# Four image layers on one core: the scan's tiles in a pool of their own, and the Toeplitz rows of two convolutions loaded into its place

## The chip, the core and the metric

The kernel runs on one core of one Trainium2 chip. The metric is device time in microseconds (us) from the start of the program to its end; it is given as the median of repeated executions. A core has five engines that run in parallel, each through its own list of instructions in order: TensorE (PE; its weight loads are shown apart as PEld), VectorE (DVE), ScalarE (ACT), GpSimd (POOL) and SyncE (SP). DMA transfers are issued from the lists of SP, ACT and POOL and run on 16 DMA engines. An engine that meets a wait in its list does nothing behind it until the wait is over.

## The reference

The input is x of 8 x 384 x 32 x 32 in f32. Four layers follow one another:

- Layer 0: an RMS norm, a selective scan over the 1,024 pixels of an image in both directions (16 states for each of 384 channels), and a gated 3x3 depthwise convolution.
- Layer 1: 1x1 and depthwise convolutions, a linear attention with 8 heads, and an MLP of width 1,536.
- Layer 2: the sum of seven depthwise convolutions, each with its batch norm.
- Layer 3: a 1x1 convolution with residual, a 13x13 depthwise convolution plus a scaled copy, and a GELU.

Cut to layers 2 and 3, in which the change mostly lies:

```
# layer 2: kernels of 13, 5, 7, 7, 3, 3, 3 with dilations 1, 1, 1, 2, 3, 4, 5
out = bn(dwconv(x, w_lk, 1))
for w, r in zip(branches, dilates):
    out = out + bn(dwconv(x, w, r))
# layer 3
y    = einsum('bchw,oc->bohw', x, pw_w)
x_pw = bn(y) + x
out  = bn(dwconv13(x_pw, dwk_w)) + bn(x_pw * dw1_w)
return gelu(out)
```

A depthwise convolution has one small kernel per channel and mixes no channels. The seven kernels of layer 2 fit into one 13x13 kernel per channel, and the scaled copy of layer 3 into the middle tap of its 13x13 kernel.

## The kernel before, in words

**Layers 0 and 1** (`_layers01`, L361 to L1119) go image by image. `front(b)` makes the inputs of the scan of image b, `scan(b)` does the scan, `layer1(b)` the rest. A loop at L1094 walks through the scan's steps, and between two steps takes pieces of `front` of the next image and `layer1` of the last one, by costs and due times (L1103 to L1115). After the last scan, `layer1` of the last image runs alone (L1117). All tiles of these layers come from one SBUF pool, `sp` (L376): among them those of the scan, `bct` (4 buffers), `rep` (6), `da` (4) and `hs` (8), each of 4 KB per partition.

Some steps of `layer1` matter below. It loads `g`, the result of the scan (L884); multiplies it with a matrix (`op`); makes the image `hh` with a border, whose two edge columns a POOL memset clears (L526) and whose middle ScalarE fills (L899); writes `hh` to DRAM (`put_image`, L532); reads it back as shifted copies `dw_i` (24 loads, L543); and ends by writing its result `xx` into the DRAM image `x2_d` from POOL (L1070), three writes for each half image.

**The convolutions** (L235 to L358) are done by TensorE with Toeplitz matrices, for all 8 images together. For one channel, the 32 rows of the image at 4 horizontal shifts fill 128 partitions. The weights for one group of taps are a 32-column matrix that holds the kernel along its diagonals; they come as windows out of a DRAM table (`g2_d`, `g3_d`), which was filled early on (`kernels`, L164). Four channels share one PSUM tile, so 384 channels make 96 groups of 32 recorded matmuls each.

`conv` (L264) takes 16 channels (four groups) as a block. For each block:

- POOL loads the block's image rows into `xt` (L281, 626 KB); two VectorE copies make the other three shifts (L289).
- SP and ACT load the windows into `tp` (L287), four transfers of 256 KB, two from each queue.
- TensorE does the groups (L301), and `put` takes the result of each out of PSUM, which has six tiles for it (`cps`).

`xt` and `tp` have three buffers each. In the first convolution ("a", layer 2), `put2` copies each group from PSUM into `yt`, ScalarE and VectorE in turn (L315, L317), and POOL writes four groups at once to `y2_d` (L319). In the second ("b", layer 3), `put3` applies GELU on ScalarE into one of three tiles `ot` (L353), and POOL writes each to the output (L354).

Between the two is the pointwise stage (L326 to L347): SP loads `yp` from `y2_d` (L328), TensorE multiplies (L333), ScalarE and VectorE finish, and POOL writes `xp_d` (L347), the image that convolution b reads. Its bias `pbias` is computed by 18 recorded matmuls before convolution a (L251 to L262).

**What sets the order.** The tile framework records the program, plans the order of each engine's list, and places the tiles of a pool in SBUF. A tile that reuses a buffer waits for the last user of that buffer. A pool that takes the place of a closed one waits, with the default setting, for the users of the closed pool as a whole. In the built program each transfer of POOL also waits for the POOL transfer eight before it, and each of SP and ACT for the one of the same queue four before it, in the convolutions.

Of the kernel before, what the change touches and what calls it, by code (L numbers as in the profile page):

```python
# [10 lines left out]
FP = mybir.dt.float32  # L11
AF = mybir.ActivationFunctionType
ALU = mybir.AluOpType
# [3 lines left out]
P = 128  # L17
C = 384
NC = C // P
H = 32  # L20
# [17 lines left out]
IMG = (H + 2) * (W + 2)  # L38

N_A6, N_T2, N_S2, N_W, N_IM = 7, 9, 3, 4, 8  # L40
N_REP, N_DA, N_HS = 6, 4, 8
AHEAD = 5000
TP = H * KT
# [24 lines left out]
def tile_layers(  # L68
# [78 lines left out]
    def bns(name, c):  # L147
        i = _BN.index(name)
        return bn_s[:, c, i : i + 1]
# [14 lines left out]
    def kernels(small, large):  # L164
# [60 lines left out]
        with nc.allow_non_contiguous_dma(reason="384 biases"):  # L225
            nc.gpsimd.dma_start(bias_d.rearrange("(c p) -> p c", p=P), bias3[:, :, 0])
            nc.gpsimd.dma_start(biasq_d, bias_d.rearrange("(g q) -> q g", q=4))
        yield 1

    _layers01(tc, nc, B, xv, x2_d, dram, ident, mean_w, eps5, eps6, one, half, minus1, vec, bns, bnt,  # L230
              rs, rsm, inproj_t, xproj_t, dtproj_t, outproj_t, taps1, taps3, taps3b, sel, alog,
              cw1_t, cw2_t, qkv_t, proj_t, w1, w2, headmask, mask8, mask8_t, kernels)


    NQ = C // 4  # L235
    GB = 4
    with tc.tile_pool(name="cw", bufs=1) as cwp, tc.tile_pool(name="cx", bufs=2) as cxp, tc.tile_pool(
        name="cps", bufs=6, space=PSUM
    ) as cps:
        xos = []  # L240
        for i in range(3):
# [5 lines left out]
        gbias = cwp.tile([P, NQ], FP, tag="gbias", name="gbias")  # L247
        for q in range(4):
            nc.scalar.dma_start(gbias[q * H : (q + 1) * H, :], biasq_d[q, :].partition_broadcast(H))

        pbias = cwp.tile([P, NC, 1], FP, tag="pbias", name="pbias")  # L251
        for m in range(NC):
            ps = cps.tile([P, HALF], FP, tag="cv", name=f"pb_{m}")
            for k in range(NC):
                nc.tensor.matmul(
                    ps[:, 0:1], pwt[:, k, m * P : (m + 1) * P], bias2[:, k, :],
                    start=(k == 0), stop=(k == NC - 1),
                )
            nc.vector.scalar_tensor_tensor(
                pbias[:, m, :], ps[:, 0:1], bns("pw", m), bnt("pw", m), ALU.mult, ALU.add  # L260
            )
            nc.vector.tensor_add(pbias[:, m, :], pbias[:, m, :], bias2[:, m, :])  # L262

        def conv(g_d, src_d, tag, put):  # L264

            NCH = 4 * GB
            xt = tp = None
            for g in range(NQ):  # L270
                if g % GB == 0:
                    xt = cxp.tile([P, NCH, RL], FP, tag="xt", name=f"xt_{tag}_{g}", bufs=3)
                    tp = cxp.tile([P, NCH, TP], FP, tag="tp", name=f"tp_{tag}_{g}", bufs=3)

                    q0 = g // GB % 2 * 2
                    at = [H * ((q0 + e) % NSH) for e in range(NSH)]
                    src = bass.AP(
                        src_d.tensor, src_d[4 * g, 0, 0].offset,
                        [[RL, H], [H * RL, NCH], [1, RL]],
                    )  # L280
                    nc.gpsimd.dma_start(xt[at[0] : at[0] + H], src)  # L281
                    for e in range(NSH):
                        win = bass.AP(
                            g_d.tensor, g_d[4 * g, e, 0, 0].offset,
                            [[KT, H], [NSH * TG * KT, NCH], [1, TP]],
                        )
                        (nc.scalar if e % 2 else nc.sync).dma_start(tp[at[e] : at[e] + H], win)  # L287
                    for n in (1, 2):
                        nc.vector.tensor_copy(  # L289
                            xt[at[n] : at[n] + n * H, :, 0 : RL - n - (n - 1)],  # L290
                            xt[at[0] : at[0] + n * H, :, n : RL - (n - 1)],
                        )
                ps = cps.tile([P, HALF], FP, tag="cv", name=f"cv_{tag}_{g}")
                for t in range(KT):
                    for e in range(4):
                        c = 4 * (g % GB) + e
                        row = xt[:, c, NSH * t : NSH * t + B * (W + PADW) - PADW]
                        rhs = bass.AP(
                            row.tensor, row.offset, [row.ap[0], [W + PADW, B], [1, W]]
                        )  # L300
                        nc.tensor.matmul(  # L301
                            ps[H * e : H * (e + 1), 0:BW],
                            tp[:, c, :].rearrange("p (j t) -> p j t", t=KT)[:, :, t], rhs,
                            start=(t == 0), stop=(t == KT - 1), skip_group_check=True,
                        )
                put(g, ps[:, 0:BW])
# [13 lines left out]

        conv(g2_d, x2_d, "a", put2)

        yf = y2_d.rearrange("(k p) h b w -> p k (h b w)", p=P)
        xf = xp_d.rearrange("(k p) h r -> p k h r", p=P)
        NB = 2 * BW
        for t in range(H // 2):  # L326
# [3 lines left out]
            for m in range(NC):  # L330
# [10 lines left out]
                for r in range(2):  # L341
# [3 lines left out]
                        yt[:, m, r * BW : (r + 1) * BW].rearrange("p (b w) -> p b w", w=W),  # L345
                    )
            nc.gpsimd.dma_start(xf[:, :, 2 * t : 2 * t + 2, :], xo)  # L347

        ov = out.rearrange("b c h w -> (c h) b w")

# [9 lines left out]

def _layers01(tc, nc, B, xv, x2_d, dram, ident, mean_w, eps5, eps6, one, half, minus1, vec, bns, bnt,  # L361
              rs, rsm, inproj_t, xproj_t, dtproj_t, outproj_t, taps1, taps3, taps3b, sel, alog,
              cw1_t, cw2_t, qkv_t, proj_t, w1, w2, headmask, mask8, mask8_t, kernels):

# [7 lines left out]
    with ExitStack() as ctx:  # L374
        wp = ctx.enter_context(tc.tile_pool(name="w0", bufs=1))
        sp = ctx.enter_context(tc.tile_pool(name="s0", bufs=2))  # L376
        accp = ctx.enter_context(tc.tile_pool(name="acc0", bufs=1, space=PSUM))
        psp = ctx.enter_context(tc.tile_pool(name="ps0", bufs=3, space=PSUM))

# [315 lines left out]
        def scan(b):  # L695
# [9 lines left out]

            def load_bc(k, r):
                d, h, _ = units[k]
                t = sp.tile([P, 2, HALF], FP, tag="bct", name=f"bct_{b}_{d}_{h}_{r}", bufs=4)
                for o in range(2):
                    src = bass.AP(  # L710
                        bc_d.tensor, bc_d[b, d, o * NST + 4 * r, h * HALF].offset,
                        [[0, 32], [L, 4], [1, HALF]],
                    )
                    nc.sync.dma_start(t[:, o, :], src)
                return t

            def load(k, i):
# [1 line left out]
                d, h, c = units[k]  # L719
                ts = []  # L720
                for src_d, n in ((dl_d, "dlt"), (v_d, "vr")):
                    t = sp.tile([P, 2 * HALF], FP, tag="rep", name=f"{n}_{b}_{d}_{h}_{c}_{i}", bufs=N_REP)
                    for j in range(2):
                        src = bass.AP(
                            src_d.tensor, src_d[b, d, P * c + 32 * (2 * i + j), h * HALF].offset,
# [35 lines left out]
            for k, (d, h, c) in enumerate(units):  # L761
                cols = bass.ts(h, HALF)
                second = k % (2 * NC) >= NC
                for r in range(NR):
# [11 lines left out]
                    end = HALF - 1 if d == 0 else 0  # L776
                    for i in range(2):
                        dlt, vt = now[i]
                        da = sp.tile([P, 2 * HALF], FP, tag="da", name=f"da_{b}_{k}_{r}_{i}", bufs=N_DA)
                        for j in range(2):  # L780
                            g = 4 * c + 2 * i + j
                            nc.scalar.activation(  # L782
# [9 lines left out]
                            sums(*late.pop(0))  # L792
                        if i == 0 and k and c == 0 and r == 0:
                            bct[NR - 1] = load_bc(k, NR - 1)
                        t = sp.tile([P, 2 * HALF], FP, tag="hs", name=f"hs_{b}_{k}_{r}_{i}", bufs=N_HS)
                        for j in range(2):
                            s = bass.ts(j, HALF)
                            k_c = carry[:, c * NR + r, 2 * i + j : 2 * i + j + 1]
# [295 lines left out]
        for b in range(B):  # L1094
            for i, _ in enumerate(scan(b)):
# [7 lines left out]
                while True:  # L1103
# [10 lines left out]
                    else:  # L1114
                        w[4] += cost  # L1115
        tick(everything=True)
        for _ in seconds[B - 1]:  # L1117
            tick()
        tick(everything=True)  # L1119


# [86 lines left out]
```

## Time and profile before

Three executions took 5239.56 us in the median (5237.00 to 5242.91).

| what | us |
|---|---|
| the profiled execution | 5247.45 |
| its span, first to last instruction | 5245.7 |
| TensorE busy | 4292.2 (82%) |
| VectorE busy | 3793.6 (72%) |
| GpSimd busy | 2911.7 (56%) |
| ScalarE busy | 2739.8 (52%) |
| the last scan's last matmul | at 4220.2 |
| layer 1 of the last image, alone | 4220 to 4558 |
| first matmul of convolution a | at 4594.75 |
| first matmul of the pointwise stage | at 4827.8 |
| first matmul of convolution b | at 4971.5 |

Times inside the profile are counted from the start of the span. A row of a group of instructions names the line, the engine and the operation, then the tile written and the tile read; after the bar it gives busy time and the mean of one, then how long the engine was idle just before it and what ended that wait. A row of waits reads "who <- whom: us in total, times, longest". A row of the timeline has start, duration, engine and line, and in brackets the idle time before it. For a DMA issued by POOL the shown duration is that of the issue; its landing is listed apart.

### The profile page before, as it was taken

What the parts mean: (1) busy time and instruction counts of PE and PEld (TensorE: products, weight loads), DVE (VectorE), ACT (ScalarE), POOL (GpSimd) and SP (SyncE); (2) the same over time, 40 slices, a digit from 0 to 9 for tenths busy, and PEclk for the clock granted to TensorE, in tenths of its full rate; (3) what the DMA queues carried; (4) which work ended last, traced back from release to release, by engine and by line L of the source; (5) the groups of instructions that cost most, each with busy time, mean ns of one, the idle gap of its engine ahead of it and who ended that gap; (6) DMA issues with size and microseconds to landing.
All of it is one profiled execution on the core that took longest, in us unless ns stands there. A gap on an engine that the chain in (4) does not pass through costs nothing. (4 is left out here: it accounts for less than half of the span.)

```text
span 5245.7 us, 57987 instructions
## 1 busy us (share of the span) xinstructions
PE 4292.2 (82%) x20128; PEld 1772.1 (34%) x20128; DVE 3793.6 (72%) x3765; ACT 2739.8 (52%) x3816; POOL 2911.7 (56%) x1472
## 2 busy tenths in 40 slices
PE   4675568888988998898889888998788879787877
PEld 1121123233333333333333333333233324365455
DVE  0399899987888788878887889788879901065344
ACT  1455544785578557755775677468536603001211
POOL 3276666676667665766675667566767800111155
PEclk7686679899989998999899999999889999899988
DMA  9866447666757674767567646765644541499698
GB/s 280 253 198 209 167 146 217 205 202 177 213 190 208 177 222 168 224 179 218 176 199 203 213 168 196 211 204 183 160 150 137 147 105 38 79 235 219 193 197 168
DMA packets 560045, 975.07 MB, mean 186 GB/s; under 512 B 53208, under 2 KB 238024, under 8 KB 559752
## 3 DMA queue, kind: packets, MB, share of 16 engines
q1 hardware_dynamic: 410992, 669.13, 42.8%
q0 software_dynamic: 56800, 205.10, 15.2%
q10 hardware_dynamic: 91960, 97.14, 6.8%
q8 instruction: 159, 2.61, 0.2%
q14 instruction: 134, 1.10, 0.1%
HBM read 726.36 MB, written 244.81 MB: 185 GB/s over the span
## 5 line engine op out<-in xcount | busy, mean ns | idle before, releaser
L808 POOL TENSOR_TENSOR hs<-hs,bct 128x1024 f32<-128x1024 f32 x768 | 2410.7, 3139 | 1001.1 <-DVE carry L804 470.6
L782 ACT ACTIVATE da<-dlt,neg_a 128x512 f32<-128x512 f32 x1536 | 1035.6, 715 | 775.7 <-DVE hs L799 718.5
L799 DVE TENSOR_TENSOR_SCAN hs<-da,du 128x512 f32<-128x512 f32 x768 | 902.4, 1209 | 248.7 <-ACT da L782 146.3
L787 DVE TENSOR_TENSOR du<-vr,bct 128x1024 f32<-128x1024 f32 x768 | 1059.3, 1379 | 29.0 <-DMA vr<-v_d 18.5
L799 DVE TENSOR_TENSOR_SCAN hs<-da,carry,du 128x512 f32<-128x512 f32 x768 | 944.1, 1267 | 56.4 <-PE acc L506 14.4
L506 PE MATMUL acc<-hs,selt 128*32 128x512 f32 x2304 | 560.5, 658 | 189.8 <-POOL hs L808 189.7
L1058 PE MATMUL mo<-hm,w 128*128 128x512 f32 x1152 | 572.0, 637 | 91.1 <-ACT hm L1056 89.4
L489 PE MATMUL mf<-ln,w 128*128 128x512 f32 x1152 | 565.6, 627 | 11.7 <-DMA w<-w_d 11.7
L501 PE MATMUL acc<-hs,selt 128*32 128x512 f32 x768 | 419.5, 645 | 72.8 <-POOL hs L808 46.8
L1058 PEld LDWEIGHTS mo<-hm,w 128*128 128x128 f32 x1152 | 219.4, 200 | 438.3 <-issue 240.3
L782 ACT ACT_TABLE_LOAD x278 | 356.7, 1283 | 7.6 <-ACT hh L899 2.7
L489 PEld LDWEIGHTS mf<-ln,w 128*128 128x128 f32 x1152 | 222.4, 200 | 334.3 <-issue 314.3
L489 PE MATMUL in<-xn,win 128*128 128x512 f32 x576 | 293.0, 640 | 12.0 <-ACT uz L603 7.7
L301 PE MATMUL cv_b<-xt_b,tp_b 128*32 128x256 f32 x3072 | 203.9, 424 | 83.3 <-ACT ot L353 60.6
L1070 POOL DMA_DIRECT2D x_d<-xx x48 | 56.4, 1177 | 350.6 <-DVE xx L1067 350.5
L289 DVE COPY xt_b<-xt_b 32x4992 f32<-32x4992 f32 (+1 forms) x48 | 135.0, 2813 | 131.8 <-DMA xt_b<-xp_d 131.0
L1056 ACT ACTIVATE hm<-mf,biasf 128x512 f32<-128x512 f32 x192 | 131.9, 687 | 179.6 <-PE mf L489 177.8
L301 PE MATMUL cv_a<-xt_a,tp_a 128*32 128x256 f32 x3072 | 182.3, 389 | 47.0 <-issue 37.1
L506 PE MATMUL dw<-dw_i,t3b 96*32 96x512 f32 x1056 | 207.5, 637 | 4.1 <-DMA dw_i<-h_d 3.6
L301 PEld LDWEIGHTS cv_b<-xt_b,tp_b 128*32 128x32 f32 x3072 | 150.8, 143 | 136.8 <-ACT ot L353 71.2
L506 PEld LDWEIGHTS acc<-hs,selt 128*32 128x32 f32 x2304 | 92.7, 114 | 301.3 <-POOL hs L808 281.0
L354 POOL DMA_DIRECT2D out<-ot x96 | 130.4, 1363 | 113.4 <-ACT ot L353 113.1
(194 smaller groups left out, 5771.4 us busy)
## 6 DMA issues: line engine op xcount, KB each, us to landing
dlt<-dl_d SPq DMA_DIRECT2D x384, 256.0 KB, 4.2
vr<-v_d SPq DMA_DIRECT2D x384, 256.0 KB, 4.9
bct<-bc_d SPq DMA_DIRECT2D x256, 256.0 KB, 3.8
ut<-u_d SPq DMA_DIRECT2D x192, 257.5 KB, 5.6
lc_i<-xn_d SPq DMA_DIRECT2D x192, 228.8 KB, 5.5
dw_i<-h_d SPq DMA_DIRECT2D x192, 228.8 KB, 4.5
w<-w_d SPq DMA_DIRECT2D x64, 576.0 KB, 6.1
w<-in_w SPq DMA_DIRECT2D x64, 576.0 KB, 5.4
```

The source lines that it names most:

```text
L289: nc.vector.tensor_copy(xt[at[n] : at[n] + n * H, :, 0 : RL - n - (n - 1)], xt[at[0] : at[0] + n * H, :, n : RL - (n - 1)],)
L301: nc.tensor.matmul(ps[H * e : H * (e + 1), 0:BW], tp[:, c, :].rearrange("p (j t) -> p j t", t=KT)[:, :, t], rhs, start=(t == 0), stop=(t = ...
L354: nc.gpsimd.dma_start(ov[g * P : (g + 1) * P], ot.rearrange("p (b w) -> p b w", w=W))
L489: nc.tensor.matmul(ps, w[:, k, m * P : (m + 1) * P], rhs[k] if isinstance(rhs, list) else rhs[:, k, :], start=(k == 0), stop=(k == NC - 1),)
L501: first = product()
L506: tc.keep_in_program_order(product())
L782: nc.scalar.activation(da[:, bass.ts(j, HALF)], dlt[:, bass.ts(j, HALF)], AF.Exp, scale=neg_a[:, g, r : r + 1],)
L787: nc.vector.tensor_mul(pairs(du), pairs(vt), bct[r][:, 0:1, :].to_broadcast([P, 2, HALF]),)
L799: nc.vector.tensor_tensor_scan(t[:, s][:, way], da[:, s][:, way], du[:, s][:, way], k_c if second else 0.0, ALU.mult, ALU.add,)
L808: made.append(nc.gpsimd.tensor_mul(pairs(t), pairs(t), bct[r][:, 1:2, :].to_broadcast([P, 2, HALF])))
L1056: nc.scalar.activation(hm, ps, AF.Gelu, bias=biasf[:, NC * i + f, :])
L1058: nc.tensor.matmul(acc[m], wb[:, f, m * P : (m + 1) * P], hm, start=(i == 0 and f == 0), stop=(i == FF // C - 1 and f == NC - 1),)
```

## The change

Four things change.

1. The scan's tiles (`bct`, `rep`, `da`, `hs`) come from a pool of their own, `scan`, placed at the right end of SBUF. It is closed when the last scan has ended. In its place a pool `win` of 20 buffers `tp` is opened, each with the windows of 8 channels (4 KB per partition).
2. During `layer1` of the last image, the first 20 window tiles of convolution a are loaded by POOL, one tile (four transfers) after each step of `layer1`. In the pointwise stage one window tile of convolution b is loaded after each of the 16 steps, by ACT and SP. Inside `conv`, windows are loaded up to ten blocks ahead.
3. `conv` takes 8 channels as a block in place of 16, with four buffers `xt` in place of three.
4. The pools of the convolutions wait tile by tile for the memory that they take over (`reuse_waits="tile"`). `pbias` is computed after convolution a.

The framework plans the order of each list anew. In the built program of the changed kernel, the windows of convolution b with numbers 0 to 19 stand in the lists of SP and ACT ahead of the pointwise stage, each behind the block of convolution a that frees its buffer.

```diff
+N_WIN, NCH = 20, 8
...
+    def load_windows(g_d, tag, n, queues):
+        if not wins:
+            wins["pool"] = ctx.enter_context(tc.tile_pool(name="win", bufs=1, side="right"))
+        tp = wins["pool"].tile([P, NCH, TP], FP, tag="tp", name=f"tp_{tag}_{n}", bufs=N_WIN)
+        for e in range(NSH):
+            at = H * ((n % 2 * 2 + e) % NSH)
+            win = bass.AP(
+                g_d.tensor, g_d[NCH * n, e, 0, 0].offset,
+                [[KT, H], [NSH * TG * KT, NCH], [1, TP]],
+            )
+            queues[e % len(queues)].dma_start(tp[at : at + H], win)
+        wins[tag, n] = tp
+
+    def windows(queues):
+        for n in range(N_WIN):
+            load_windows(g2_d, "a", n, queues)
+            yield
...
-    with tc.tile_pool(name="cw", bufs=1) as cwp, tc.tile_pool(name="cx", bufs=2) as cxp, tc.tile_pool(
-        name="cps", bufs=6, space=PSUM
+    with tc.tile_pool(name="cw", bufs=1, reuse_waits="tile") as cwp, tc.tile_pool(
+        name="cx", bufs=2, reuse_waits="tile"
+    ) as cxp, tc.tile_pool(
+        name="cps", bufs=6, space=PSUM, reuse_waits="tile"
     ) as cps:
...
         def conv(g_d, src_d, tag, put):
-            NCH = 4 * GB
             for g in range(NQ):
-                if g % GB == 0:
-                    xt = cxp.tile([P, NCH, RL], FP, tag="xt", name=f"xt_{tag}_{g}", bufs=3)
-                    tp = cxp.tile([P, NCH, TP], FP, tag="tp", name=f"tp_{tag}_{g}", bufs=3)
+                n, first = divmod(4 * g, NCH)
+                if first == 0:
+                    xt = cxp.tile([P, NCH, RL], FP, tag="xt", name=f"xt_{tag}_{n}", bufs=4)
...
+                    for m in range(n, min(n + 1 + N_WIN // 2, NB_C)):
+                        if (tag, m) not in wins:
+                            load_windows(g_d, tag, m, [nc.sync, nc.scalar])
+                    tp = wins[tag, n]
...
             nc.gpsimd.dma_start(xf[:, :, 2 * t : 2 * t + 2, :], xo)
+            if t < N_WIN:
+                load_windows(g3_d, "b", t, [nc.scalar, nc.sync])
...
+        scan_ctx = ExitStack()
+        scanp = scan_ctx.enter_context(tc.tile_pool(name="scan", bufs=1, side="right"))
...
-                t = sp.tile([P, 2, HALF], FP, tag="bct", name=f"bct_{b}_{d}_{h}_{r}", bufs=4)
+                t = scanp.tile([P, 2, HALF], FP, tag="bct", name=f"bct_{b}_{d}_{h}_{r}", bufs=4)
...
         tick(everything=True)
+
+        scan_ctx.close()
+        ahead = windows([nc.gpsimd])
         for _ in seconds[B - 1]:
             tick()
+            next(ahead, None)
+        for _ in ahead:
+            pass
         tick(everything=True)
```

The same replacement of `sp.tile` by `scanp.tile` is made for `rep`, `da` and `hs`, and the block that computes `pbias` moves behind the call of `conv` for convolution a.

## The prediction

> **What bounds the kernel now.** I read the page first (TensorE busy 82%, VectorE 72%, no engine full everywhere), then cut the span into stages, since the diff only touches what follows the last scan. The table of stages (start:end, length, then busy time of PE, PEld, DVE, ACT, POOL, TensorE clock, DMA share, GB/s):
>
> ```profile
> 4220.00:4558.00 338.00, 300.66 (x896) 129.95 (x888) 31.63 (x46) 66.32 (x107) 8.89 (x13) 0.94 0.30 70
> 4558.00:4594.70 36.70, 3.97 (x18) 3.91 (x18) 8.73 (x9) 0.00 (x0) 8.47 (x8) 0.55 0.89 135
> 4594.70:4814.00 219.30, 182.14 (x3072) 157.22 (x3072) 143.18 (x94) 17.50 (x47) 40.85 (x44) 0.98 1.11 235
> 4814.00:4827.80 13.80, 0.15 (x1) 0.00 (x0) 0.00 (x0) 0.37 (x1) 0.75 (x1) 0.62 0.77 192
> 4827.80:4953.00 125.20, 125.16 (x288) 55.30 (x288) 35.83 (x94) 36.55 (x47) 11.26 (x15) 0.99 0.65 208
> 4953.00:4971.50 18.50, 0.28 (x1) 0.01 (x1) 6.30 (x5) 0.78 (x1) 2.72 (x4) 0.62 0.64 156
> 4971.50:5240.50 269.00, 203.90 (x3072) 150.78 (x3072) 129.50 (x46) 45.01 (x95) 147.05 (x116) 0.88 0.94 179
> ```
>
> The rows are: the last image's layer 1, TensorE-bound with the DMA 30% used; an empty gap; convolution a; a gap; the pointwise stage, TensorE without a hole; a gap; convolution b. Convolution a has its DMA queues full (1.11: packets overlap, so the share can pass 1). Its TensorE needs 182 of 219 us; what it waits for is seen in the timeline of one block of 16 channels:
>
> ```profile
> 4704.24 1.25 POOL L319 DMA_DIRECT2D y_d<-yt  x1 [7.32 <-ACT yt L315]
> 4705.48 0.67 POOL L281 DMA_DIRECT2D xt_a<-x_d  x1
> ...
> 4711.36 2.73 DVE L289 COPY xt_a<-xt_a 64x4960 f32<-64x4960 f32 x1
> ...
> 4714.19 7.46 PE L301 MATMUL cv_a<-xt_a,tp_a 128*32 128x256 f32 x128 [1.43 <-issue]
> 4714.38 0.67 POOL L281 DMA_DIRECT2D xt_a<-x_d  x1
> ```
>
> TensorE starts at 4714.19, when the second VectorE copy ends (4714.09). The block's input was asked for at 4696.25, landed at 4708.1, and was copied in 6 us; with 7.5 us of matmuls and 1.6 us until the next issue this makes 27 us for a ring of three buffers, 8.9 us a block. So convolution a is a closed loop of input loads under a saturated DMA. Convolution b is another loop; its waits, summed:
>
> ```profile
> ACT ot L353 <- DMA out<-ot: 175.0, 67, 9.7
> PEld cv_b L301 <- ACT ot L353: 71.2, 22, 5.8
> PE cv_b L301 <- ACT ot L353: 60.6, 21, 5.3
> ```
>
> ScalarE waits for one of three output tiles to be written, TensorE for ScalarE. Landings (KB each, median us), from the list of DMA issues:
>
> ```profile
> xt_a<-x_d POOLq DMA_DIRECT2D x24, 626.0 KB, 11.9
> xt_b<-xp_d POOLq DMA_DIRECT2D x24, 626.0 KB, 9.5
> x_d<-xx POOLq DMA_DIRECT2D x48, 256.0 KB, 16.1
> out<-ot POOLq DMA_DIRECT2D x96, 128.0 KB, 7.5
> ```
>
> In the last 23 us, with no loads in flight, the median of out is 3.0.
>
> **What the skill says.** "DMA: Bandwidth & Descriptors", section "Issuing engines are not separate DMA queues": all issuers share 16 DMA engines. The trace agrees: three queues together fill the share to 1.11. So loading earlier helps only if there is room earlier. Section "Queues, rings and completion order": an engine goes round its queues and takes each ring in order. That fits an input load which follows a y_d write on POOL landing in 11.9 us, against a least of 5.6. Section "Anatomy of one DMA": some 2 us are fixed; out alone at 3.0 agrees, so half the size is not half the landing. "SBUF — State Buffer", section "SBUF: two separate sides": VectorE's f32 copies lock POOL out of writing descriptors. POOL's out issues agree: 0.887 us median, 1.363 mean, 3.456 most, beside the L289 copies.
>
> **The change, part by part.** The sum is against the profiled execution: 5247.45 us (span 5245.7); the median of the three runs is 7.9 lower, and I carry the difference over.
>
> *Scan pool.* In the built program the order of every engine is the same until the last scan ends: 0 us. The moved tiles keep their numbers.
>
> *Eighty window loads on POOL in layer 1.* Each carries 32x8x128 f32, 128 KB. POOL has 8.9 us of work in those 338, so it is free, but its order matters: 28 loads stand before the memset of hh_1 and 12 more before that of hh_0 (L526), and each load waits for the POOL transfer eight before it. Issue: no row of this shape; out (1,024 pieces) takes 0.887 and g_d (128) 0.588, so about 0.62; 80 x 0.62 = 50 us of issue. Four can go at 4224, four more when the x_d and g_d writes land (4235 to 4239), then, with eight in flight and about 5.5 us each, 1.4 per us: hh_1's memset near 4254, hh_0's near 4263. The writes of hh that need them start at 4262.40 and 4270.13, so the memsets are just in time. The loads share the DMA with layer 1's own chain: the g load of 4236 (6.1 us, +2), the hh writes (4.7 us, +1), and 24 dw_i loads (5.6 MB in 24 us at a share of 0.71, +4). Cost 7 us; bounds 0 and 25 (memsets late too). After 4320 the stage has no DMA pressure and POOL's next work is at 4487.
>
> *The start of convolution a.* The timeline before it:
>
> ```profile
> 4556.27 3.44 POOL L1070 DMA_DIRECT2D x_d<-xx  x3 [61.30 <-DVE xx L1067]
> 4574.45 4.86 POOL L243 MEMSET xo<- 128x1878 f32 x3 [14.74 <-issue]
> 4579.27 1.95 POOL L281 DMA_DIRECT2D xt_a<-x_d  x3
> 4586.82 8.31 DVE L289 COPY xt_a<-xt_a 32x4992 f32<-32x4992 f32 x3 [1.55 <-DMA xt_a<-x_d]
> 4594.75 5.56 PE L301 MATMUL cv_a<-xt_a,tp_a 128*32 128x256 f32 x60 [9.93 <-DMA tp_a<-g_d]
> ```
>
> Everything waits for the last x_d write at 4574.3. With waits by tile two memsets go earlier; the third still waits for that write in the built order. Then: 4574.3 + 1.7 memset + 4.6 landing (half the bytes, windows no longer beside it; 5.6 is the least of the full size) + 2 x 1.4 copies + 0.4 = 4583.8, against 4594.7: -10.9. The pbias matmuls (4 us) move into the next gap of 13.8, covered by the y_d landing of 8 us.
>
> *Convolution a.* Twenty windows are ready, but the built order shows where the freed buffers lead: the next window is issued as soon as one block is done, and after the 28 that convolution a lacks come 20 of convolution b, all ahead of the pointwise stage. So 48 windows still pass during 48 blocks, one per block as before (24 x 2), and the queues stay full. The loads are twice as many, half as large. The input loop has four buffers of 8 channels; the later of two blocks has a y_d write ahead: 0.5 copy + 0.9 + 0.7 issue + about 9 landing (y_d's 512 KB and 313 KB in one ring, where 512 + 626 took 11.9) + 3.3 copies + 3.8 matmuls = 18.2, over four = 4.55 us a block. 48 x 4.55 = 218, less 3 for the first blocks = 215: -4. Bounds: the matmuls alone, 182 (-37), and a landing as long as before (+35). ScalarE's y copies stand behind its window issues, which wait for loads two blocks older; that is inside the same balance.
>
> *Gap.* SP's yp load stands behind the last windows: +1.2. Pointwise stage: nothing is added to it, since the hoisted windows are past: 0. *Gap to b:* half a load (-1.3) and half the copies (-2.7): -4.
>
> *Convolution b.* Only 28 windows remain, so the last 20 blocks have none. POOL's order is now regular: input, two outs. The load of block n is issued after out 2n-5, so six outs fit one turn: 0.9 + 0.7 + L + 3.0 copies + 3.8 matmuls + 0.8 = 9.2 + L. L is some 6.4 with windows (half of 9.5 is 4.8, plus two outs ahead), 4.3 without: 2.6 and 2.25 us an out. The out loop itself: (0.5 + 0.3 + 0.9 + 5.4) / 3 = 2.4, below it. 28 x 5.2 + 20 x 4.5 = 236, plus 2 for the ends: 238 against 269: -31. Bounds: -80 (TensorE, 1.9 an out) and +32 (L stays 9.6).
>
> Sum: +7 - 10.9 - 4 + 1.2 - 4 - 31 = -41.7, so 5205.7 profiled and 5239.6 - 41.7 = 5198 median.
>
> **Rivals.** *B, TensorE-bound convolutions.* If windows only ever yield to inputs, a falls to 190 and b to 215: +4 - 10.9 - 29 - 4 - 54 = -94, about 5146. For it: windows have twenty blocks of slack. Against: ScalarE and SP throttle on them. *C, the out round trip stays.* Three ot tiles are unchanged; if b keeps 266, only the edges are won: 5226. For it: 175 us of that wait. Against: half of each input ahead in the ring goes. *D, slower.* Four buffers of 8 channels hold 32 where three of 16 held 48. If a landing does not shrink with its size (the fixed part, the queue), the loop takes its place: L of 11 in a gives (18.2 + 2) / 4 = 5.05, 242 us (+23); 8.8 in b gives 3.0 an out, 288 (+19): 5275. It decides from about L = 10 in a and 8 in b. *E, memsets late.* POOL's queue holds hh back by 20 more: 5218. That the change does nothing is excluded: the order differs.
>
> **How the numbers follow.** Chances: likeliest 0.48 (own range 5165 to 5230), B 0.12, C 0.18, D 0.15, E 0.07. Low 5152 leaves out about half of B, high 5258 the worse two thirds of D: some 0.16 together. A measurement of this kernel tells 0.2% (10.5 us) from no change: faster 0.75 (all of B, nearly all of the likeliest and of E, 0.11 of C), same 0.07, slower 0.18 (D and a rest).
>
> **What would show it.** Right: tp_a loads on POOL from about 4224, convolution a starting some 4 us earlier, at about 4.5 us a block with the share still over 1; no window load during the pointwise stage; convolution b speeding up in its last 20 blocks. Wrong: hh written after 4275; xt landings above 10 us; the wait for out still near 175 us.

## The result and the profile after

The changed kernel takes 5225.75 us in the median of 19 executions (5214.55 to 5241.32), the kernel before, run beside it, 5241.16 (5231.19 to 5252.17). The ratio is 0.9973, with a 95% interval of 0.9965 to 0.9982: it is faster by some 14 us, a third of the 41 that I had forecast. The profiled execution took 5218.79 us (span 5217.0).

The same table of stages as before the change, for the changed kernel (start:end, length, then busy time of PE, PEld, DVE, ACT, POOL, TensorE clock, DMA share, GB/s):

```profile
4214.80:4577.80 363.00, 306.73 (x896) 129.83 (x888) 31.45 (x46) 66.34 (x107) 56.59 (x95) 0.92 0.45 95
4577.80:4602.80 25.00, 0.00 (x0) 0.00 (x0) 2.91 (x3) 0.00 (x0) 7.21 (x7) 0.54 0.71 99
4602.80:4814.90 212.10, 184.44 (x3072) 158.08 (x3072) 156.13 (x142) 17.49 (x47) 69.26 (x67) 0.98 1.07 241
4814.90:4824.80 9.90, 2.35 (x25) 2.13 (x19) 0.92 (x6) 0.37 (x1) 0.76 (x1) 0.70 0.78 218
4824.80:4950.50 125.70, 125.70 (x288) 55.38 (x288) 35.76 (x94) 36.53 (x47) 11.26 (x15) 0.98 0.66 207
4950.50:4964.60 14.10, 0.26 (x1) 0.00 (x0) 3.67 (x5) 0.78 (x1) 3.09 (x5) 0.67 0.58 158
4964.60:5212.00 247.40, 192.77 (x3072) 160.44 (x3072) 143.07 (x94) 45.16 (x96) 148.05 (x139) 0.94 0.80 168
```

The first row is 25 us longer than before (338), the pointwise stage is as long as it was (125.2 before), and every other row is shorter. With exact ends (the scan's last matmul, the end of the last x_d write's issue, the first and last matmul of a stage) the differences are: layer 1 alone +23.4, the start of convolution a -10.0, a -7.1, gap -3.9, pointwise +0.5, gap -4.3, convolution b -21.9. That is -23; another 5 of the two profiles' difference lie before the end of the last scan, where the lists are the same, and I take them for the spread between executions.

Where layer 1 lost it is seen in stretches of 20 us from the end of the last scan. Kernel before, then changed kernel (columns as above):

```profile
4220.20:4240.20 20.00, 8.50 (x26) 3.34 (x18) 3.31 (x5) 0.00 (x0) 3.52 (x8) 0.84 0.88 97
4240.20:4260.20 20.00, 15.75 (x34) 7.05 (x35) 2.25 (x3) 1.38 (x2) 0.00 (x0) 0.82 0.21 55
4260.20:4280.20 20.00, 10.09 (x24) 3.93 (x22) 0.00 (x0) 2.75 (x4) 0.00 (x0) 0.86 0.46 150
4280.20:4300.20 20.00, 18.99 (x106) 4.48 (x108) 0.00 (x0) 2.34 (x4) 0.00 (x0) 0.88 0.74 216
```

```profile
4214.80:4234.80 20.00, 8.51 (x26) 3.34 (x18) 3.32 (x5) 0.00 (x0) 7.11 (x11) 0.84 0.99 97
4234.80:4254.80 20.00, 11.44 (x21) 5.02 (x22) 2.23 (x3) 0.00 (x0) 14.02 (x26) 0.65 1.04 202
4254.80:4274.80 20.00, 14.69 (x35) 6.20 (x33) 0.03 (x1) 4.13 (x6) 13.23 (x25) 0.95 1.05 222
4274.80:4294.80 20.00, 4.85 (x6) 0.55 (x6) 0.00 (x0) 0.00 (x0) 11.29 (x20) 0.50 1.05 248
```

The next-to-last column (the DMA share) is what to look at: the DMA, at 0.21 to 0.88 before, is now full (0.99 to 1.05) for 80 us, and TensorE, which in the fourth stretch had 19 us of work, has 4.9. The list of DMA issues, from the scan's end to 115 us later (KB each, median us from issue to landing), says who waits. The kernel before, over the same stretch, then the changed kernel:

```profile
dw_i<-h_d SPq DMA_DIRECT2D x24, 228.8 KB, 4.6
h_d<-hh ACTq DMA_DIRECT2D x2, 816.0 KB, 4.7
```

```profile
tp_a<-g_d POOLq DMA_DIRECT2D x80, 128.0 KB, 7.2
dw_i<-h_d SPq DMA_DIRECT2D x24, 228.8 KB, 5.4
h_d<-hh ACTq DMA_DIRECT2D x2, 816.0 KB, 10.7
```

The writes of hh, 4.7 us in the median before, take 10.7. The second of them, which the first dw_i load waits for, takes 13.2 in place of 5.8. Of the dw_i loads (4.6 before) those that go out while window loads are still issued take 13.0, the later ones 5.2. Counted from the end of the last scan, the first activation of hh, which comes behind the g load and its matmuls, starts at 41.2 us instead of 35.7, the second write of hh at 54.9 instead of 49.3, the first dw_i load at 68.2 instead of 55.1, and the 1x1 convolution behind them at 106.2 instead of 82.4. It was not the memsets of hh in POOL's list. The timeline of the changed kernel around them:

```profile
4252.75 0.30 POOL L551 MEMSET hh<- 128x48 f32 x2
...
4262.99 0.30 POOL L551 MEMSET hh<- 128x48 f32 x2
...
4269.52 0.69 ACT L924 ACTIVATE hh<-h,bias 128x512 f32<-128x512 f32 x1 [1.89 <-PE h L514]
4270.29 0.38 ACTq L557 DMA_DIRECT2D h_d<-hh  x1
```

Each pair is done before the activations of its image begin (4256.65 and 4264.37), and the write that the dw_i loads wait for goes out at once when the last activation ends (4270.21).

The start of convolution a, in the timeline of the changed kernel (start, length, what it waited for before):

```profile
4574.36 3.44 POOL L1095 DMA_DIRECT2D x_d<-xx  x3 [61.31 <-DVE xx L1092]
4577.79 3.28 POOL L268 MEMSET xo<- 128x1878 f32 x2
4592.30 1.66 POOL L268 MEMSET xo<- 128x1878 f32 x1 [11.23 <-DMA x_d<-xx]
4593.91 2.33 POOL L290 DMA_DIRECT2D xt_a<-x_d  x4
4599.82 5.90 DVE L296 COPY xt_a<-xt_a 32x2496 f32<-32x2496 f32 x4 [24.04 <-DMA xt_a<-x_d]
4602.81 2.80 PE L308 MATMUL cv_a<-xt_a,tp_a 128*32 128x256 f32 x24 [27.82 <-DVE xt_a L296]
```

Two memsets ahead of the wait, one behind it, and TensorE starts 10.5 us after the last write lands: the order is as worked out, the time 1 us longer (9.5). In convolution a the inputs, half as large, land in 8.1 us in the median (11.9 before). The waits of convolution b, summed (us, times, longest):

```profile
ACT ot L376 <- PE cv_b L308: 146.0, 70, 16.7
...
DVE xt_b L296 <- DMA xt_b<-xp_d: 93.9, 39, 7.3
...
ACT ot L376 <- DMA out<-ot: 41.7, 20, 6.2
```

ScalarE's wait for an output tile fell from 175.0 to 41.7. VectorE's wait for an input, 120.0 before, is 93.9 and now the larger of the two.

### The profile page after: what moved, and what is told of

Its sections match the earlier page's. It is cut to its first block, busy times and chain, and to the rows that moved or that the text cites. A ratio compares the mean times of both kernels' runs of the same rounds, so it can differ in the third digit from the quotient of the medians.

```text
span 5217.0 us, 58464 instructions
## 1 busy us (share of the span) xinstructions
PE 4288.4 (82%) x20128; PEld 1783.5 (34%) x20128; DVE 3813.8 (73%) x3861; ACT 2740.1 (53%) x3816; POOL 2988.6 (57%) x1600
## 5 line engine op out<-in xcount | busy, mean ns | idle before, releaser
L514 PE MATMUL mf<-ln,w 128*128 128x512 f32 x1152 | 564.4, 626 | 10.9 <-DMA w<-w_d 10.9
L514 PE MATMUL in<-xn,win 128*128 128x512 f32 x576 | 293.9, 642 | 13.2 <-ACT uz L628 8.8
L308 PE MATMUL cv_b<-xt_b,tp_b 128*32 128x256 f32 x3072 | 192.8, 404 | 68.2 <-DVE xt_b L296 36.6
L296 DVE COPY xt_b<-xt_b 32x2496 f32<-32x2496 f32 x96 | 146.0, 1521 | 109.4 <-DMA xt_b<-xp_d 103.1
## 6 DMA issues: line engine op xcount, KB each, us to landing
lc_i<-xn_d SPq DMA_DIRECT2D x192, 228.8 KB, 5.4
dw_i<-h_d SPq DMA_DIRECT2D x192, 228.8 KB, 4.5
```

Of the source, the lines that this page charges most:

```text
L296: nc.vector.tensor_copy(xt[at[e] : at[e] + e * H, :, 0 : RL - e - (e - 1)], xt[at[0] : at[0] + e * H, :, e : RL - (e - 1)],)
L308: nc.tensor.matmul(ps[H * e : H * (e + 1), 0:BW], tp[:, c, :].rearrange("p (j t) -> p j t", t=KT)[:, :, t], rhs, start=(t == 0), stop=(t = ...
L514: nc.tensor.matmul(ps, w[:, k, m * P : (m + 1) * P], rhs[k] if isinstance(rhs, list) else rhs[:, k, :], start=(k == 0), stop=(k == NC - 1),)
```

## The experiments

My theory after this: the window loads right after the scan fill the DMA while a short chain of transfers sets the end of layer 1, and this is the whole loss; in convolution b the pace is set by the input loads, which take their turn in GpSimd's list behind the output writes ("outs" below). The experiments ran in three rounds on three chips: e1 to e4 on the one numbered 7, e5 to e8 on 8, e9 and r1 to r3 on 9. The kernel before takes 5286, 5283 and 5286 us there in the median; each ratio is to the kernel before on the same chip. The stages below are read from one profile each with the same ends as above (us).

| kernel | layer 1 alone | start of a | a | gap | pointwise | gap | b | ratio, interval |
|---|---|---|---|---|---|---|---|---|
| before, first profile | 339.0 | 35.0 | 219.4 | 13.6 | 125.5 | 18.2 | 269.0 | |
| before, again (r1) | 343.3 | 38.8 | 222.5 | 13.6 | 125.9 | 18.1 | 269.7 | |
| changed, first profile | 362.4 | 25.0 | 212.3 | 9.7 | 126.0 | 13.9 | 247.1 | 0.9973, 0.9965 to 0.9982 |
| changed, again (r2) | 368.7 | 27.9 | 216.1 | 11.5 | 126.6 | 13.9 | 249.0 | |
| changed, third (r3) | 369.3 | 27.6 | 213.0 | 9.7 | 125.5 | 13.9 | 250.3 | |
| e1, loads held back | 342.2 | 27.3 | 217.4 | 10.3 | 126.6 | 14.0 | 247.4 | 0.9923, 0.9907 to 0.9939 |
| e2, half blocks alone | 343.4 | 34.1 | 214.7 | 11.4 | 126.5 | 13.9 | 258.9 | 0.9955, 0.9937 to 0.9972 |
| e3, six inputs | 370.1 | 28.3 | 218.2 | 11.6 | 125.8 | 13.7 | 246.7 | 0.9973, 0.9961 to 0.9984 |
| e4, six outputs | 367.9 | 28.0 | 219.5 | 10.7 | 125.7 | 13.9 | 251.6 | 0.9975, 0.9963 to 0.9987 |
| e5, b's inputs on SP | 368.2 | 27.6 | 219.8 | 9.6 | 126.1 | 13.2 | 225.8 | 0.9935, 0.9924 to 0.9947 |
| e6, e1 and all inputs on SP | 342.3 | 23.7 | 232.4 | 11.5 | 125.4 | 12.8 | 227.1 | 0.9893, 0.9880 to 0.9906 |
| e7, half the loads early | 347.4 | 27.6 | 216.8 | 9.8 | 126.0 | 14.1 | 259.9 | 0.9935, 0.9920 to 0.9949 |
| e8, none early | 343.5 | 29.9 | 256.3 | 9.8 | 125.4 | 13.9 | 260.1 | 1.0000, 0.9991 to 1.0008 |
| e9, e1 and b's inputs on SP | 342.1 | 28.1 | 214.3 | 9.8 | 126.3 | 13.1 | 228.2 | 0.9884, 0.9864 to 0.9904 |

**e1: the same loads, later in layer 1.** One number of the key-value sums is copied by GpSimd into each window tile before its loads, and the loop asks for the loads only from there on:

```diff
         tp = wins["pool"].tile([P, NCH, TP], FP, tag="tp", ...)
+        if gate is not None:
+            nc.gpsimd.tensor_copy(tp[0:1, 0, 0:1], gate)
 ...
             ks = t2(f"ks_{b}")
+            if b == B - 1:
+                mark["g"] = wp.tile([1, 1], FP, tag="gate", name="gate")
+                nc.gpsimd.tensor_copy(mark["g"], kv[PR : PR + 1, 0:1])
```

> The changed kernel, with 77 of the 80 early window loads held back: each window tile is first touched by a GpSimd copy of one number that exists only when the attention's key-value sums are done (about 140 us after the last scan), so the loads run in the second half of layer 1, which had almost no transfers. Theory (the early loads fill the DMA queues while layer 1's short chain g load, hh writes, dw_i loads needs them, and this cost 23 us where I had 7): layer 1 alone, 361.9 us with the change, returns to 338 to 345; hh writes land in about 5 us again, dw_i loads in about 5; everything from convolution a on stays as in the changed kernel (within 5 us); in all 17 to 23 us less than the changed kernel, about 5205, ratio to the kernel before about 0.993. Rival (the loss comes from the scan tiles' pool of their own, from its hand-over, or from the profile's spread and not from the loads): layer 1 alone stays at 355 to 365, about 5225.

Layer 1 alone came to 342.2 (e3 and e4, with the changed kernel's early loads on the same chip: 370.1 and 367.9), the later stages stayed within some 5 us, and the ratio went from 0.9973 to 0.9923. In the first 115 us after the scan the DMA issues of this kernel show

```profile
dw_i<-h_d SPq DMA_DIRECT2D x24, 228.8 KB, 4.4
h_d<-hh ACTq DMA_DIRECT2D x2, 816.0 KB, 4.7
```

and the stretch that had fallen to 4.9 us of TensorE work is back at 15.9, with the DMA at 0.71:

```profile
4311.80:4331.80 20.00, 15.87 (x93) 4.75 (x95) 0.00 (x0) 1.75 (x3) 0.00 (x0) 0.81 0.71 204
```

The loads themselves, all but three issued from 4398.9 to 4462, leave layer 1 as long as in the kernel before (342.2 against 343.3). The rival, the pool's hand-over, is out: the pool is the same here.

**e7: half of them early.** The dose between the two:

```diff
-            load_windows(g2_d, "a", n, queues, mark["g"])
+            load_windows(g2_d, "a", n, queues, mark["g"] if n >= 10 else None)
```

> The changed kernel with half the dose: ten of the twenty window tiles (40 loads) go right after the last scan as there, the other ten wait until the key-value sums are done. Theory (contention, in proportion to the loads that share the time with layer 1's chain): these 40 loads are through by about 45 us after the scan, ahead of the dw_i loads, so the g load and the hh writes are still slowed and the dw_i loads are not: layer 1 alone at 348 to 356, between 342 (none early) and 368 (all early) on that chip; ratio to the kernel before about 0.995. Rival (the first loads alone do the harm, through GpSimd's order or the g load): 362 or more, ratio 0.997. Rival 2 (only the dw_i loads suffer): 342 to 345, ratio 0.9925.

Layer 1 alone: 347.4. So 43 early loads (three of the others slip ahead, as in e1) cost 5 us, all 80 cost 27. The harm isn't in proportion to the bytes. The issues of this kernel in the same 115 us:

```profile
tp_a<-g_d POOLq DMA_DIRECT2D x43, 128.0 KB, 7.4
dw_i<-h_d SPq DMA_DIRECT2D x24, 228.8 KB, 4.3
h_d<-hh ACTq DMA_DIRECT2D x2, 816.0 KB, 6.5
```

The last early load goes out 54 us after the scan; the dw_i loads start 10 us later and are untouched. What is lost is lost before the hh writes (first activation of hh at 44.6 us, 39.8 in e8, which has no early loads and ran on the same chip). The second hh write lands after 5.9 us here, as in the kernel before. The dear loads are those that overlap the hh writes and the dw_i loads. My expectation was 348 to 356, so it missed by little, between theory and second rival. Convolution b took 259.9 in this one profile although its lists in b equal those of e1; what that is stays open (see r1 to r3). The ratios leave little room for such 12 us: 0.9935 is e1's 0.9923 plus 6 us, with an interval of some 8 us to either side.

**e8: none early.** The first 20 windows wait for the last result of layer 1 and are then asked for by the convolution itself:

```diff
+        if tag == "a" and n < N_WIN:
+            nc.vector.tensor_copy(tp[:, 0, 0:1], mark["g"])
 ...
-        ahead = windows([nc.gpsimd])
         for _ in seconds[B - 1]:
             tick()
-            next(ahead, None)
```

> The changed kernel with no window load ahead of the convolution: all 48 of convolution a are asked for only when the last image's layer 1 has its last result (VectorE touches each of the first 20 window tiles with one number that exists only then), from SyncE and ScalarE; blocks, buffers and waits by tile as in the changed kernel, and convolution b's windows still loaded as buffers come free. Theory (most of the gain came from blocks of half the size, the early loads cost more than they brought): layer 1 alone 341 to 346 on that chip, the start of convolution a 30 to 36 (27.3 with the loads late in layer 1), a at 218 to 228, b 247 to 250; ratio to the kernel before 0.994 to 0.996, that is better than the changed kernel's 0.9973 and 5 to 18 us worse than the first experiment's 0.9923. Rival (loads ahead are what speeds the convolutions): a above 230, ratio at or above 0.9973.

Here the rival was right: a took 256.3, the ratio is 1.000. The code asks for eleven windows at the first block, and ScalarE's half of that burst stands ahead of its y copies. Its timeline (start, length, wait before), and the sum of ScalarE's waits for windows up to the end of a:

```profile
4612.76 27.13 ACTq L248 DMA_DIRECT2D tp_a<-g_d  x15
4639.99 0.37 ACT L325 COPY yt<-cv_a 128x256 f32<-128x256 f32 x1 [65.88 <-DMA tp_a<-g_d]
```

```profile
ACT yt L325 <- DMA tp_a<-g_d: 156.4, 21, 65.9
```

In e1 the same wait is 24.6 us, 6 times. The first hole is the smaller part: the first eight blocks took 43.6 us against e1's 35.2, and the rest of the loss is spread over the whole of a. So with this deep ring, asked for from ScalarE's and SyncE's lists, the loads ahead are needed; what they must not do is start right after the scan. The lack of loads ahead alone is not it: e2 has six window buffers, no loads ahead and 214.7 us in a. From none early to late in layer 1 (e8 to e1) is worth 0.77%, some 41 us, and the profiles place 39 of it in a (they show another 13 in b, more than the medians leave room for).

**e2: half blocks alone.** The kernel before, with blocks of 8 channels, four input and six window buffers:

```diff
-            NCH = 4 * GB
+            NCH, GC = 8, 2
...
-                    xt = cxp.tile(..., bufs=3)
-                    tp = cxp.tile(..., bufs=3)
+                    xt = cxp.tile(..., bufs=4)
+                    tp = cxp.tile(..., bufs=6)
```

> The kernel before, with one thing of the change alone: the convolutions' blocks are 8 channels instead of 16, with four input buffers and six window buffers; no own pool, no loads ahead of the stages, no waits by tile. Theory (convolution b gained by half-size input loads and copies, of which the load and its copies are a shorter turn, and by the absence of windows in its last 20 blocks): here all windows pass during the convolutions, so b gets only the first of these: about 255 of 269 (in the changed kernel 247), convolution a within 5 of its 219, the start of a about 4 earlier, layer 1 as before (338): about 5222, ratio 0.996. Rival 1 (b gained only because windows were held ahead): b stays at 265 to 272, ratio 1.000. Rival 2 (half blocks alone give all of b's 22): b at 247, ratio 0.995.

Against the kernel before (r1, on another chip): start -4.7, a -7.8, the gaps -6.4, b -10.8, layer 1 unchanged, and a ratio of 0.9955. So about half of b's gain is the block size (258.9 where I had expected 255). The other half lies in the last 20 blocks: they take 5.33 us each in e2, whose windows pass to the end of b, and 4.63 to 4.88 in the changed kernel, e1 and e3, whose windows are through by then; the first 28 take 5.44 and 5.34 to 5.59. This one edit, without pool and early loads, is at 0.9955 against the whole change's 0.9973; the intervals overlap, so that it is better is not shown.

**e3 and e4: more buffers.** `bufs=6` for `xt` in place of 4, and `bufs=6` for `ot` in place of 3:

> The changed kernel with six input buffers of 8 channels in the convolutions instead of four. Theory (the turn of the input buffers, load, landing, two copies, matmuls, sets the pace of both convolutions): the last 36 outputs of convolution b, 85 us with the change, go to TensorE's own pace of about 1.9 to 2.0 us each (70), the part with windows falls by some 10 more, b about 222 of 247; convolution a, whose DMA share is 1.07, gains less, 5 to 15 of 212. In all some 30 us less than the changed kernel, ratio to the kernel before about 0.991. Rival (ScalarE's wait for an output tile, three buffers, sets b's pace; in a the DMA is full): b within 4 of 247, a within 4 of 212, ratio 0.997.

> The changed kernel with six output tiles in convolution b instead of three. Theory (the input buffers set the pace): b gains 0 to 4 of 247, though ScalarE's wait for an output (41.7 us) goes, and the wait of VectorE for input loads grows; ratio 0.997. Rival (the round trip of the output tiles sets it): b falls by 15 to 25, ratio about 0.993.

Neither moved b: 246.7 and 251.6, ratios 0.9973 and 0.9975. e4's ratio fell out as my theory had it: ScalarE's wait for an output tile is gone and b isn't shorter (but VectorE's wait for inputs, 94.4, did not grow). e3 did not: 246.7 is the rival's number. But e4 speaks against that rival's cause, the output tiles; and VectorE's wait for inputs in e3 is unchanged:

```profile
DVE xt_b L296 <- DMA xt_b<-xp_d: 93.9, 41, 7.2
```

With six buffers GpSimd's list in b is the same as with four, input, out, out, input. The loads were not held by a buffer but by what stands ahead of them.

**e5: b's inputs from another queue.**

```diff
-                    nc.gpsimd.dma_start(xt[at[0] : at[0] + H], src)
+                    (nc.sync if tag == "b" else nc.gpsimd).dma_start(xt[at[0] : at[0] + H], src)
```

> The changed kernel, with the input loads of convolution b alone issued from SyncE instead of GpSimd. Six input buffers moved nothing (b 246.7), and in that kernel the order of GpSimd's list (an input load, two outs, an input load) was the same as before, so the buffers had not let a load go earlier. Theory (the turn that sets b's pace goes through GpSimd's order: the input load of a block stands behind the out of five outputs before, six outs a turn): with the loads on another queue VectorE's wait for inputs (93.9 us) goes below 50, the last blocks come to 3.9 to 4.2 us each instead of 4.7, b falls to 220 to 232, ratio to the kernel before about 0.992. Rival 1 (three output tiles): the wait for an output takes the input's place and b stays above 240. Rival 2 (the transfers themselves, landing slower as more are in flight): landings of inputs grow from 4.9 to above 7, b above 240, ratio 0.997.

b fell to 225.8, in the range, and the ratio to 0.9935, 20 us below the changed kernel's (I had 0.992). Waits of b in this kernel:

```profile
ACT ot L376 <- DMA out<-ot: 77.4, 37, 4.7
DVE xt_b L296 <- DMA xt_b<-xp_d: 57.8, 23, 4.1
```

VectorE's wait fell by 36 us (to 57.8, not below 50), and ScalarE's for an output tile came back: the next limit. Counting outputs in the two timelines, from the first matmul of b on: the changed kernel's first 8 outputs take 18.3 us, the next 8 take 28.2; here 17.8 and 14.5. In the changed kernel, TensorE does the four blocks that were loaded ahead and a fifth, then waits for the sixth, whose load was issued behind outs at 4978.09:

```profile
4964.66 20.38 PE L308 MATMUL cv_b<-xt_b,tp_b 128*32 128x256 f32 x320 [13.90 <-DVE xt_b L296]
...
4972.70 1.41 POOL L290 DMA_DIRECT2D xt_b<-xp_d  x1
...
4978.09 1.66 POOL L290 DMA_DIRECT2D xt_b<-xp_d  x1
...
4989.43 9.41 PE L308 MATMUL cv_b<-xt_b,tp_b 128*32 128x256 f32 x128 [4.40 <-DVE xt_b L296]
```

**e6 and e9: the two gains together.** e1 with `nc.sync` for the inputs of both convolutions, and e1 with the line of e5:

> The early window loads held back until the attention's key-value sums are done, as in the first experiment, and the input loads of both convolutions on SyncE. Theory: layer 1 alone as there (342 on that chip); convolution a, where the input no longer stands behind a y write, falls from 217 to about 200 to 210, no lower since its DMA share is over 1; b falls to 220 to 232; in all ratio to the kernel before 0.984 to 0.988. Rival (a queue in common with the windows holds the inputs on SyncE back as the writes did on GpSimd): a at 215 or more, b above 240, ratio 0.992 as in the first experiment.

> The window loads held back until the key-value sums are done, and the input loads of convolution b alone on SyncE; those of convolution a stay on GpSimd. Theory (the two gains are in different stages and add; convolution a lost 15 in the kernel with both on SyncE, since windows stood behind inputs in one queue): layer 1 alone 342, a 215 to 220, b 224 to 230; ratio to the kernel before 0.985 to 0.988. Rival (the ratio of that kernel, 0.989, is what both together can give): 0.989 to 0.992.

e9 adds up: layer 1 342.1, b 228.2, ratio 0.9884, 61 us below the kernel before and 47 below the changed one. It is the lowest ratio here, though its interval overlaps that of e6. The ratio fell between my range and the rival's; the stages are about those that I had given. In e6 the ratio, 0.9893, lay between my range and the rival's: b came out as I had it, but a went up to 232.4, the rival's way. That windows stood behind inputs in SP's list I only argued: the trace shows that SP's first window load in a comes at 4632.5, 22 us after ScalarE's, and a DMA share of 0.90 where e9 has 1.07. e9, with a's inputs back on GpSimd, has 214.3.

**r1 to r3: the spread.**

> The kernel before once more, for the spread of its stages between executions. If convolution b's share of the change is 22 us as in the first two profiles: b at 266 to 272 here. If b varies by some 13 us with the clock that TensorE is granted (two kernels with the same order of work in b took 247.4 at a mean clock near 0.92 and 259.9 near 0.89): b anywhere from 255 to 272, and layer 1 alone, a and the pointwise stage within 3 of the first profile, adjusted to the chip.

> The changed kernel once more, for the spread of its stages. Layer 1 alone 362 to 370, convolution a 212 to 220. If b is fixed by its queues alone: 247 plus or minus 3. If the granted clock moves it: 245 to 262, the longer the lower the clock of the stretch with windows.

> The changed kernel a third time, as above: layer 1 alone 362 to 370; b 247 plus or minus 3 if its queues alone fix it, 245 to 262 if the granted clock moves it.

Layer 1 alone, 343 against 369 and 369, and b, 269.7 against 249.0 and 250.3, repeat the first pair: +26 and -20 (250.3 is just over the 247 plus or minus 3 expected from the queues alone). Seven profiles have the same lists in b. Five of them (three of the changed kernel, e1 and e3) take 246.7 to 250.3; e7 and e8 take 259.9 and 260.1. Most of these 10 us lie in the first 28 blocks, 5.8 us each in both, and TensorE's mean clock in b was 0.89 and 0.91 there, 0.92 to 0.96 in the five. Both ran on chip 8, and e1, e3, r2 and r3 did not, so the chip may be the cause as well as the single execution; no run here tells. The gain from SyncE's queue does not depend on it: e9 against r2 and r3, all on chip 9, shows 21 to 22 us.

## Why the prediction was right and wrong

Its sum was +7 - 10.9 - 4 + 1.2 - 4 - 31 = -41.7. The second pair of profiles (r1 against the mean of r2 and r3) gives, in the same order, +25.7 - 11.1 - 8.0 - 3.0 - 4.2 - 20.1, and +0.1 in the pointwise stage: -20.6. The timed executions say -14, with an interval of 9 to 18. The 6 us between them can't be placed: before the last scan's end the lists are the same, and that end comes anywhere from 4235.6 to 4252.4 us in the profiles of the experiments. In the items below the forecast stands first, then what was measured.

- **The scan pool** cost nothing in layer 1: with it and without the early loads (e1), the stage is as before within 1 us. A cost before the end of the last scan would be hidden in the spread just named.
- **Eighty window loads in layer 1, +7: the step that failed.** It measured +23 to +26. The places were right (g load, hh writes, dw_i loads), and each was priced too low. Between the marks of the table below: up to the first activation of hh (the g load) +2, measured 4 to 5.5; from there to the first dw_i load (the hh writes) +1, measured 7 to 7.5; from there to the 1x1 convolution (the dw_i loads) +4, measured 11 to 15. The prediction gives no working for the +2, +1 and +4. I had read the mean share of 0.30 as room, and even under the dw_i loads, where I had a share of 0.71, I charged a few us for a stream that kept eight loads in flight for 80 us with the share at 0.99 to 1.05. The hh writes and the dw_i loads that met it landed at 2 to 3 times their time, 4.7 to 10.7 and 4.6 to 13.0; the window loads themselves took 7.2 us where I had 5.5. The section of the Trainium skill that the prediction cites for shared DMA engines ("DMA: Bandwidth & Descriptors", "Issuing engines are not separate DMA queues") says that the transfers of all issuers run on the same 16 DMA engines and interleave, and this trace agrees: GpSimd's stream slowed ScalarE's writes and SyncE's loads. I named it for layer 1 too, and priced it too low. My bound of 25 was the right size, for a wrong reason: I had it for late memsets, rival E, and these were in time.

| us after the last scan | before (r1) | changed (r2, r3) | e7, half early | e1, held back |
|---|---|---|---|---|
| first activation of hh | 40.0 | 44.2, 44.1 | 44.6 | 40.6 |
| second write of hh | 53.6 | 57.9, 57.8 | 58.3 | 54.2 |
| first dw_i load | 59.4 | 71.2, 70.5 | 64.2 | 59.9 |
| 1x1 convolution behind them | 86.9 | 112.1, 113.0 | 91.1 | 85.8 |

- **The start of a, -10.9:** right, -10.0 and -11.1. e2 shows that the half blocks alone give 5 of it; e8, with waits by tile and no window ahead, 9.
- **Convolution a, -4:** -7 to -8. The share stayed over 1 and a block takes 4.42 us where I had 4.55; the landing was 8.1 where I had about 9.
- **The gaps, +1.2 and -4:** -3.0 to -3.9, and -4.3. The first went the other way: SP's yp load was not late (issued 5.1 us after the last matmul of a, 8.9 before). The pointwise stage had no window load and did not change, as said.
- **Convolution b, -31:** -20 to -22. This is the second term that was mis-sized, by 9 to 11. The cause was right: the first 28 blocks took 5.36 us each (I had 5.2), the last 20 took 4.86 (4.5), together 11 more, of which I had put 2 at the ends. e3, e4 and e5 confirm that it is the turn through GpSimd's list and not the number of buffers. What I left out is that the turn starts late: four blocks are loaded ahead, the loads of the next stand behind the first outs, and a hole of some 8 us against the later pace follows, which e5 removes. In the last blocks the inputs landed in 4.6 us where I took 4.3.
- **Rivals.** B (TensorE-bound) is out: TensorE needs 184 of 212 and 193 of 247. (B's sum has +4 where the parts give +7 and +1.2, which moves it by 4 us.) C (the out round trip stays) is out: 41.7 us of that wait, and six output tiles change nothing. That its total, 5226, is the measured 5225.75 is luck: it kept b at 266 and layer 1 at +7, two errors that nearly cancel. D is out: the inputs land in 8.1 and 5.1. E had the total nearly right (5218), too, for a cause that the trace excludes.
- **The signs.** Of those named for being right, window loads on POOL from the scan's end (4218.4), 4.42 us a block in a with the share over 1, no window load in the pointwise stage and faster last blocks in b came; the earlier start of convolution a did not: it came 8 us later (4602.81), since layer 1 ended later. None of the signs of being wrong came: the second hh write was issued at 4270.29, before the 4275 named. What was late was its landing, at 4283.5 against 4275.9 in the kernel before. One reading was off without weight: POOL's next work after the memsets in the kernel before is at 4491.5, not 4487.

The direction came from gains in four places, which held, and a fifth that I had as a loss. Of the 21 us by which the stages fell short of the forecast, layer 1 is some 19 and b 11, less 9 that a and the gaps gave beyond theirs.

## What to carry to other kernels

A stage's mean DMA share did not tell what the share was at the moment at which a new stream of loads started (0.30 against 0.21 to 0.88 in stretches of 20 us): cut the stage finely, find the short transfers that its chain waits for, and tie the prefetch to a result that exists only after them (here 27 us, by a copy of one number). When a wait for a load is long, look at what stands ahead of that load in its queue's list before adding buffers: six buffers gave nothing, another queue gave 20 us. A deep ring of prefetched tiles also needs to be filled before its stage starts: in e8, where ScalarE and SyncE filled it inside the stage, ScalarE's copies waited behind the loads and the stage took 39 us more.

## What the runs showed of the hardware beyond this

- A stream of 128 KB loads, eight in flight, more than doubled the landing of transfers from other queues: an 816 KB write from 4.7 to 10.7 us, 228.8 KB loads from 4.6 to 13.0 while it lasted. Within GpSimd's own queue, the three window loads of e1 that went out right behind the x_d and g_d writes landed after 21.0 us, the other 77 after 5.8.
- TensorE's granted clock changes within one loop. In e7's convolution b, TensorE did 243 matmuls at a clock of 0.84 in a stretch of 21.6 us in which the last windows were loaded, and 305 at 1.00 in a later one without window loads:

```profile
5130.20:5151.80 21.60, 16.62 (x243) 11.96 (x238) 11.06 (x8) 3.69 (x8) 11.38 (x12) 0.84 0.79 160
...
5173.40:5195.00 21.60, 17.57 (x305) 15.85 (x308) 14.68 (x10) 4.26 (x9) 15.96 (x15) 1.00 0.59 124
```

  Over all of b the mean clock was 0.89 there, and 0.94 in e1, which has the same lists and 12.5 us less. Whether the clock made the gaps or the gaps the clock, these runs don't tell.
